# A Perceiver block with one core: splitting the first loads, moving late weights behind the query stores, and folding queries in runs of 1 KB

## The chip, the cores and the metric

One core of a Trainium2 chip runs the whole block in one launch. The metric is the device time of that launch in microseconds; the median of three runs is compared. The core's engines work side by side, each through its own instructions in order: PE (matrix products into PSUM banks, with PEld its weight load), DVE (vector work), ACT (functions and copies), POOL (here the reductions over partitions) and SP, which issues most of the DMAs. An engine waits for another only through semaphores. DMAs of one issuing order are kept to eight lanes: a DMA waits until the eighth before it has landed.

## The reference, cut to what matters

```python
def _L0_xattn_ref(query, context, w_q, w_kv, w_out, b_out):
    q = query @ w_q
    k, v = jnp.split(context @ w_kv, 2, axis=-1)
    ...
    scores = jnp.einsum('bhqd,bhkd->bhqk', q, k) * SCALE
    attn = jax.nn.softmax(scores, axis=-1)
    out = jnp.einsum('bhqk,bhkd->bhqd', attn, v)
    ...
    return out @ w_out + b_out
...
x = x + _L0_xattn_ref(_layernorm(x, axis=-1), ctx_768, ...)
x = x + _L0_attn_ref(_layernorm(x, axis=-1), ...)
x = x + _L0_ffn_ref(_layernorm(x, axis=-1), ...)
```

x is 32 x 64 x 256, the context 32 x 1601 x 192, with 16 heads of 64. The second term is a time mixing (three products with Wk, Wv and Wr, a scan over the 64 steps with a decay per channel, a product with Wo), the third a feed-forward net of width 1024. All is float32.

## The kernel before, in words

**Folded queries.** The key weights are not applied to the context. They are folded into the queries: for each head the query (64 numbers) is multiplied by the head's key weights (192 x 64), so that scores are products of a folded query with the raw context, over 192 channels. The setup makes these folded queries for all 32 batch rows and stores them in DRAM (q_dram, 25.2 MB). It works on four groups of eight rows (512 tokens). For each group, `queries` normalises x (statistics L110, xn L177), transposes it (xnT), and then for each pair of head pairs makes the queries on PE (q_ps L195), has ACT scale them into qT (L202), multiplies them by the turned key weights wkT (ql_ps L211 for the first 128 channels, qh_ps L226 for the other 64), has DVE and ACT copy the results to q_lo and q_hi (L218, L219, L233, L234) and issues their stores on SP (L236, L242). q_lo and q_hi have two buffers each.

**Loads of the setup.** SP issues first x_sb's tiles 0 to 3 (L91), then the key weights wk_lo and wk_hi in halves, the other tiles of x_sb, the first context's blocks cb (twelve DMAs, L153), and then everything that is used later: the value weights wv_lo and wv_hi, wo_sb, the four time-mixing weights nat_*, biases and per-channel columns (L281 to L298). ACT issues the two halves of wq_sb (L275). The time-mixing weights are turned on PE at the end of the setup (L320) and copied by DVE (L325), and the decay rows are made there (L327 to L332).

**Halves.** After the setup a loop runs over 64 halves u: batch row b = u // 2 and half of the heads j = u % 2. Half u computes its scores (`scores`: six groups of 24 s_ps matmul rows, L466, into two banks, each group copied to s_sb by ACT, L473, with a running maximum on DVE, L475 and L477; then a rest, L485) and the maximum over all keys (L495 and L496 on DVE, then a reduction on POOL, L503). Then come, for the half before it, the products of its probabilities with the context (`av_lo`, o_lo L569, thirteen steps; `av_hi`, o_hi L583), then the subtraction of the maximum (L513, DVE) and the exponential (L514, ACT) of its own scores, in four parts. So the exponentials of one half are covered by PE's products of the half before. The first half has none before it: its parts are put into the score loop of half 1 as hooks (L673), behind the copies of groups 2, 3, 4 and 5.

**Context.** `ctx_prep` turns the blocks cb of the next row into cT on DVE (L260, L261) and moves a part of it by DMA (L262); `ctx_load` loads the plain context c (L133, L136), and `q_load` the folded queries of a row (L163). `fill` names work that is put between steps of `av_lo`.

The kernel is written against a framework that assigns each instruction its place in its engine's order by a plan of its own; the order of the text is a priority, not the final order. Pools give memory out in the order in which they are opened: what is opened after the setup takes the setup's memory, and waits for its last readers.

Of the kernel before, what the change touches and what calls it, by code (L numbers as in the profile page):

```python
# [9 lines left out]
F32 = mybir.dt.float32  # L10
AF = mybir.ActivationFunctionType
ALU = mybir.AluOpType
# [3 lines left out]
P = 128  # L16
# [4 lines left out]
def kernel(  # L21
# [35 lines left out]
    nc = tc.nc  # L57

    B, T, D = x.shape
    NK, C = ctx_768.shape[1:]  # L60
# [30 lines left out]
    nc.sync.dma_start(x_sb[:, 0:4, :], xr[:, 0:4, :])  # L91
# [25 lines left out]
    with ExitStack() as st_b:  # L117
        with ExitStack() as st_a:
            kp = st_a.enter_context(tc.tile_pool(name="keys", bufs=2))
            cpool = st_a.enter_context(tc.tile_pool(name="ctx", bufs=1))  # L120
            aw = st_a.enter_context(tc.tile_pool(name="aw", bufs=1))
            wv_lo = aw.tile([P, INNER], F32, name="wv_lo")
            wv_hi = aw.tile([P, INNER], F32, name="wv_hi")
            wo_sb = aw.tile([P, INNER // P, D], F32, name="wo_sb")
# [44 lines left out]
            def queries(tg, sp, sps, wq_sb, wkT):  # L169
# [19 lines left out]
                for g in range(NP // 2):  # L189
                    qT = sp.tile([P, 2, TG], F32, tag="qT", name=f"qT_{tg}_{g}", bufs=6)  # L190
                    for k in range(2):
                        hp = 2 * g + k
                        pq = sps.tile([P, TG], F32, tag="ps", name=f"q_ps_{tg}_{hp}")
                        for c in range(2):
                            nc.tensor.matmul(  # L195
                                pq,
                                lhsT=wq_sb[:, c, hp * P : (hp + 1) * P],
                                rhs=xnT[:, c, :],
                                start=(c == 0),
                                stop=(c == 1),  # L200
                            )
                        nc.scalar.activation(qT[:, k, :], pq, AF.Copy, scale=HD**-0.5)  # L202
                    lo = sp.tile([P, QB, 4, T], F32, tag="q_lo", name=f"q_lo_{tg}_{g}", bufs=2)
                    hi = sp.tile([P, QB, 2, T], F32, tag="q_hi", name=f"q_hi_{tg}_{g}", bufs=2)
                    for k in range(2):
                        pl = [
                            sps.tile([P, QB, T], F32, tag="f", name=f"ql_ps_{tg}_{g}_{k}_{o}", bufs=6)
                            for o in range(2)
                        ]
                        for o in range(2):  # L210
                            nc.tensor.matmul(  # L211
                                pl[o],
                                lhsT=wkT[o * HD : (o + 1) * HD, 2 * g + k, 0:P],
                                rhs=qT[o * HD : (o + 1) * HD, k, :],
                                start=True,
                                stop=True,
                            )
                        nc.vector.tensor_copy(lo[:, :, 2 * k, :], pl[0])  # L218
                        nc.scalar.copy(lo[:, :, 2 * k + 1, :], pl[1])  # L219
                    ph = [  # L220
                        sps.tile([P, QB, T], F32, tag="f", name=f"qh_ps_{tg}_{g}_{o}", bufs=6)
                        for o in range(2)
                    ]
                    for k in range(2):
                        for o in range(2):
                            nc.tensor.matmul(  # L226
                                ph[o][k * C2 : (k + 1) * C2, :, :],
                                lhsT=wkT[o * HD : (o + 1) * HD, 2 * g + k, P:C],
                                rhs=qT[o * HD : (o + 1) * HD, k, :],
                                start=True,  # L230
                                stop=True,
                            )
                    nc.vector.tensor_copy(hi[:, :, 0, :], ph[0])  # L233
                    nc.vector.tensor_copy(hi[:, :, 1, :], ph[1])  # L234
                    ns = slice(4 * g * T, (4 * g + 4) * T)
                    nc.sync.dma_start(  # L236
                        q_dram[tg][:, 0:P, ns].rearrange("b p n -> p b n"),
                        lo.rearrange("p b h t -> p b (h t)"),
                    )
                    for k in range(2):  # L240
                        ns = slice((4 * g + 2 * k) * T, (4 * g + 2 * k + 2) * T)
                        nc.sync.dma_start(  # L242
                            q_dram[tg][:, P:C, ns].rearrange("b p n -> p b n"),
                            hi[k * C2 : (k + 1) * C2].rearrange("p b h t -> p b (h t)"),
                        )
# [19 lines left out]
            with tc.tile_pool(name="setup", bufs=1) as sp, tc.tile_pool(  # L265
# [7 lines left out]
                for n in range(2):  # L273
                    ns = slice(n * INNER // 2, (n + 1) * INNER // 2)
                    nc.scalar.dma_start(wq_sb[:, :, ns], wqr[:, :, ns])  # L275
                    nc.sync.dma_start(wk_lo[:, ns], w_kv[0:P, ns])
                    nc.sync.dma_start(wk_hi[:, ns], w_kv[P:C, ns])
# [3 lines left out]
                nc.sync.dma_start(wv_lo, w_kv[0:P, INNER : 2 * INNER])  # L281
                for r0 in (0, C2):
                    nc.sync.dma_start(wv_hi[r0 : r0 + C2, :], w_kv[P:C, INNER : 2 * INNER])
                nc.sync.dma_start(wo_sb, w_out.rearrange("(c p) n -> p c n", p=P))
                nats = {}
                for n, w in (("Wk", Wk), ("Wv", Wv), ("Wr", Wr), ("Wo", Wo)):
                    nats[n] = sp.tile([P, 2, D], F32, name=f"nat_{n}")
                    nc.sync.dma_start(nats[n], w.rearrange("(c p) h -> p c h", p=P))
                for n, v in enumerate((b_out, bo, b2)):
                    nc.sync.dma_start(bias_rows[:, n, :], v.partition_broadcast(P))  # L290
                with nc.allow_non_contiguous_dma(reason="per-channel vectors"):
                    for n, v in enumerate((time_decay, time_first)):
                        nc.sync.dma_start(cols[:, n, :], v.rearrange("(c p) -> p c", p=P))
                    for n, v in enumerate((mix_k, mix_v, mix_r)):
                        nc.sync.dma_start(
                            cols[:, 2 + n, :], v.rearrange("a b (c p) -> p (a b c)", p=P)
                        )
                    nc.sync.dma_start(b1_sb, b1.rearrange("(c p) -> p c", p=P))  # L298

# [16 lines left out]
                for n, nat in nats.items():  # L316
                    ps = sps.tile([P, 2, D], F32, tag="ps", name=f"rw_ps_{n}")
                    for hc in range(2):
                        for oc in range(2):
                            nc.tensor.transpose(  # L320
                                ps[:, hc, oc * P : (oc + 1) * P],
                                nat[:, oc, hc * P : (hc + 1) * P],
                                ident,
                            )
                    nc.vector.tensor_copy(rw_T[n], ps)  # L325

                nc.vector.tensor_scalar(omm, cols[:, 2:5, :], -1.0, 1.0, ALU.mult, ALU.add)  # L327
                nc.scalar.activation(td, cols[:, 0, :], AF.Exp)
                nc.scalar.activation(td, td, AF.Exp, scale=-1.0)
                for c in range(2):  # L330
                    nc.vector.tensor_scalar(
                        td_rows[:, c, :], ones, td[:, c : c + 1], None, ALU.mult  # L332
                    )

# [5 lines left out]
            def bank(shape, name):  # L340
                return ps_m.tile(shape, F32, tag="m", name=name)

# [315 lines left out]
            for u in range(2 * B):  # L658
# [5 lines left out]
                if phase == 1 and i >= 0:  # L664
                    fill = {2: [out.yproj], 6: [older.out] if i else []}
                elif phase == 2 and i >= 0:
                    fill = {6: [mixer.mix]}
                elif phase == 3 and i >= 0:
                    fill = {3: [mixer.project], 9: [mixer.gate]}

                if u == 1:

                    hooks = {i + 2: [part] for i, part in enumerate(parts)}  # L673
                elif last is not None:
                    hooks = {3: [last.inverse]}
                    last.total()
                else:
                    hooks = {}
# [4 lines left out]
                mb = max_all(u, mx)  # L683
                if last is not None:
                    last.av_lo(fill)
# [6 lines left out]
                if j == 0 and b + 1 < B:  # L692
                    cT_next = ctx_prep(b + 1)
                elif j == 1:
                    cT = cT_next
# [154 lines left out]
```

## Time and profile before

| | us |
|---|---|
| runs | 2626.71, 2626.44, 2626.01; median 2626.44 |
| profiled execution, its own time | 2624.3 |
| its span | 2622.5, mean granted clock 0.997 |
| first matmul on PE | 8.91 |
| first q_ps matmul | 17.04 |
| first store of q_lo issued | 38.77 |
| last store of q_hi issued (L242) | 139.60, over 1.57 |
| first copy of scores to s_sb | 147.40 |
| last qh_ps matmuls of the setup | 132.36, over 1.09 |
| first o_lo matmul | 186.44 |

The profile lists an operation as line, engine, operation, output and input tile, shape and count, with the busy time, the mean of one in ns and what ended the engine's idle time before it. Start times are from the start of the span. "SPq" stands for the queue of SP: the time that it needs to issue a DMA. From issue to landing the stores took 8.6 us (q_lo, 1 MB) and 6.8 us (q_hi, 256 KB) in the median. A group of transposes of a time-mixing weight (L320, four of 128 x 128) took 0.60 to 0.89 us on PE, a copy of the result (L325) 0.69 us on DVE.

### The profile page before, as it was taken

How to read it: one execution, taken by the hardware profiler on the slowest of the kernel's cores; microseconds unless marked ns; L12 is line 12 of the kernel's file. 1: busy time of each engine (PE TensorE's matmuls, PEld its weight loads, DVE VectorE, ACT ScalarE, POOL GpSimd, SP SyncE). 2: the span in 40 equal slices, each digit the busy share in tenths (PEclk: the TensorE clock that was granted, in tenths of full speed). 3: DMA queues.
4: the chain of work that ended last, by engine and by line, in shares of the span. 5: the costliest groups of instructions: out<-in, count | busy, mean ns of one | idle time of the engine just before them, and what ended most of it. 6: DMA issues, size and time to landing. Idle time of an engine off the chain costs nothing.

```text
span 2622.5 us, 28521 instructions
## 1 busy us (share of the span) xinstructions
PE 2593.2 (99%) x11456; PEld 1217.1 (46%) x11456; DVE 1907.2 (73%) x2283; ACT 953.6 (36%) x1019; POOL 355.3 (14%) x176
## 2 busy tenths in 40 slices
PE   8989999999999999999999999999999999999999
PEld 3334444444444444444444444444444444444466
DVE  4458878777787878777787868777787868787741
ACT  2333334333333334343433333343433334343221
POOL 0011111111111111111111111111111111111100
PEclk9989999999999999999999999999999999999999
DMA  8983333233322323333331313333331323310100
GB/s 202 284 162 57 56 51 63 44 63 63 63 57 49 63 39 63 44 63 63 63 63 44 63 39 63 46 61 63 63 63 44 63 45 57 59 29 20 51 11 23
DMA packets 437781, 169.33 MB, mean 65 GB/s; under 512 B 332400, under 2 KB 423952, under 8 KB 437648
## 3 DMA queue, kind: packets, MB, share of 16 engines
q1 hardware_dynamic: 437104, 166.46, 32.9%
q8 instruction: 90, 1.47, 0.3%
q10 hardware_dynamic: 544, 1.05, 0.1%
q14 instruction: 43, 0.35, 0.0%
HBM read 138.60 MB, written 27.26 MB: 63 GB/s over the span
## 4 chain that ended last, share of the span: by engine, by line
PE 96%; DMA 2%; SPq 1%; DVE 1%; POOL 0%; issue 0%; ACT 0%; DVEq 0%; POOLq 0%; ACTq 0%
PE s_ps L466 37%; PE o_lo L569 28%; PE o_hi L583 13%; PE s_ps_r L485 3%; PE fy L775 2%; PE v_ps L629 2%; PE y_ps L642 2%; PE h_ps L761 2%; PE q_ps L195 2%; PE o_hi L593 1%; PE ql_ps L211 1%; DMA q_dram<-q_lo 1%; PE Wv_ps L383 1%; PE Wr_ps L383 1%; PE Wk_ps L383 1%; DMA q_dram<-q_hi 1%
## 5 line engine op out<-in xcount | busy, mean ns | idle before, releaser
L466 PE MATMUL s_ps<-q,cT 64*128 64x512 f32 x4608 | 1011.3, 594 | 8.6 <-ACT s_sb L473 7.8
L569 PE MATMUL o_lo<-s_sb,c 128*128 128x512 f32 (+1 forms) x1664 | 743.5, 596 | 0.0
L473 ACT COPY s_sb<-s_ps 128x1024 f32<-128x1024 f32 x384 | 388.6, 1012 | 958.6 <-PE s_ps L466 945.5
L466 PEld LDWEIGHTS s_ps<-q,cT 64*128 64x128 f32 x4608 | 442.6, 188 | 548.9 <-issue 537.9
L514 ACT ACTIVATE s_sb<-s_sb 128x2048 f32<-128x2048 f32 (+1 forms) x256 | 398.6, 1585 | 466.0 <-DVE s_sb L513 466.0
L513 DVE TENSOR_TENSOR s_sb<-s_sb,mb 128x2048 f32<-128x2048 f32 (+1 forms) x256 | 471.6, 1886 | 101.9 <-POOL mb L503 101.9
L569 PEld LDWEIGHTS o_lo<-s_sb,c 128*128 128x128 f32 (+1 forms) x1664 | 307.5, 190 | 358.1 <-issue 350.8
L477 DVE TENSOR_TENSOR m<-m,s_sb 128x1024 f32<-128x1024 f32 x256 | 313.6, 1225 | 180.1 <-ACT s_sb L473 168.2
L583 PE MATMUL o_hi<-s_sb,c 128*64 128x512 f32 x1536 | 342.9, 595 | 0.0
L546 POOL PARTITION_ALL_REDUCE den<-sum x64 | 207.4, 3240 | 834.9 <-DVE oT L609 673.2
L540 DVE TENSOR_TENSOR t<-t,s_sb 128x1024 f32<-128x1024 f32 x256 | 310.5, 1213 | 4.0
L503 POOL PARTITION_ALL_REDUCE mb<-mx x64 | 114.2, 1785 | 906.7 <-DVE mx L496 788.7
L583 PEld LDWEIGHTS o_hi<-s_sb,c 128*64 128x64 f32 x1536 | 105.3, 137 | 220.0 <-issue 197.2
L556 DVE STREAM_TRANSPOSE turned<-den 128x512 f32<-128x512 f32 x64 | 45.5, 711 | 221.3 <-POOL den L546 221.3
L485 PE MATMUL s_ps_r<-q,cT 64*65 64x256 f32 x768 | 93.6, 376 | 0.0
L260 DVE STREAM_TRANSPOSE cT<-cb 128x768 f32<-128x768 f32 x96 | 92.7, 967 | 0.0
L475 DVE TENSOR_TENSOR m<-s_sb 128x1024 f32<-128x1024 f32 x64 | 75.8, 1184 | 10.3 <-ACT s_sb L473 10.3
L485 PEld LDWEIGHTS s_ps_r<-q,cT 64*65 64x65 f32 x768 | 54.0, 134 | 52.8 <-issue 33.5
L538 DVE TENSOR_TENSOR t<-s_sb 128x1024 f32<-128x1024 f32 x64 | 77.5, 1211 | 0.0
L102 POOL TENSOR_TENSOR rstd_ln<-rstd_ln,root 128x1 f32<-128x1 f32 (+1 forms) x24 | 31.3, 1304 | 276.5 <-DVE rstd_ln L101 276.5
L195 PE MATMUL q_ps<-xnT,wq_sb 128*128 128x512 f32 x128 | 61.0, 616 | 0.0
L642 PE MATMUL y_ps<-wo_sb,outT 128*128 128x256 f32 x256 | 58.0, 379 | 0.0
(111 smaller groups left out, 1507.4 us busy)
## 6 DMA issues: line engine op xcount, KB each, us to landing
q<-q_dram SPq DMA_DIRECT2D x64, 768.0 KB, 6.6
c<-in_ctx_dram SPq DMA_DIRECT2D x32, 1152.0 KB, 6.2
cb<-in_ctx_dram SPq DMA_DIRECT2D x192, 104.0 KB, 4.2
cb<-in_ctx_dram SPq DMA_DIRECT2D x192, 96.0 KB, 3.3
q_dram<-q_lo SPq DMA_DIRECT2D x16, 1024.0 KB, 8.6
q_dram<-q_hi SPq DMA_DIRECT2D x32, 256.0 KB, 6.8
x_sb<-in_x_dram SPq DMA_DIRECT2D x4, 512.0 KB, 9.7
w_sb<-in_L_ffn_w_dram SPq DMA_DIRECT2D x2, 1024.0 KB, 5.0
```

The costliest lines, as they stand in the source:

```text
L195: nc.tensor.matmul(pq, lhsT=wq_sb[:, c, hp * P : (hp + 1) * P], rhs=xnT[:, c, :], start=(c == 0), stop=(c == 1),)
L466: nc.tensor.matmul(ps[:, k, :], lhsT=cT[rs, s, i * P : (i + 1) * P], rhs=q[rs, s, js : js + HALF], start=(s == 0), stop=(s == NS - 1),)
L473: nc.scalar.copy(s_sb[:, 2 * i : 2 * i + 2, :], ps)
L477: nc.vector.tensor_tensor(m2, m2, s_sb[:, 2 * i : 2 * i + 2, :], ALU.max)
L485: nc.tensor.matmul(ps[0:KR, k, 0:HH], lhsT=cT[rs, s, NB1 * BL : KT + 1], rhs=q[rs, s, js + k * HH : js + (k + 1) * HH], start=(s == 0), st ...
L503: nc.gpsimd.partition_all_reduce(mb, mx, P, bass_isa.ReduceOp.max)
L513: nc.vector.tensor_tensor(s, s, m, ALU.subtract)
L514: nc.scalar.activation(s, s, AF.Exp)
L540: nc.vector.tensor_tensor(t2, t2, p[:, 2 * i : 2 * i + 2, :], ALU.add)
L546: nc.gpsimd.partition_all_reduce(self.den, self.sum, P, bass_isa.ReduceOp.add)
L569: nc.tensor.matmul(self.po, lhsT=self.ctx[0:n, self.at[c], 0:P], rhs=self.s_sb[0:n, c, :], start=(c == 0), stop=(c == NCK - 1),)
L583: nc.tensor.matmul(self.ph[o * C2 : (o + 1) * C2, :], lhsT=self.ctx[:, self.at[c], P:C], rhs=self.s_sb[:, c, :], start=(c < 2), stop=False ...
```

## The change

1. **First loads.** x_sb's tiles 0 to 3 are loaded in two halves, one on SP and one on ACT, between the first and the second half of the key weights; wk_hi and half of wq_sb move between the queues too.
2. **Folded queries.** Two pairs of head pairs are handled together: four query products, then the two q_lo, then one q_hi of twice the size, whose runs in DRAM are 1 KB instead of 512 B. There are half as many stores of q_hi.
3. **Late loads.** Value weights, wo_sb, time-mixing weights, biases and columns are issued after the setup's block in the text. Their pool is opened there, so wv_lo, wv_hi and wo_sb take memory of the setup. The time-mixing weights are loaded as halves into tiles of the time mixing.
4. **Weights turned.** The four time-mixing weights are turned in `av_lo` of half 1 (the fill of u = 2, behind steps 2, 5, 8 and 11), and copied by ACT instead of DVE. The decay rows are named in the fill of u = 3.
5. **First exponentials.** The hooks of half 1 move to the copies of groups 3, 4 and 5 (the last has two parts). `ctx_prep(1)` moves from half 0 behind the maximum of half 1.

```diff
-    nc.sync.dma_start(x_sb[:, 0:4, :], xr[:, 0:4, :])
...
-                for g in range(NP // 2):
-                    qT = sp.tile([P, 2, TG], F32, tag="qT", name=f"qT_{tg}_{g}", bufs=6)
+                for e in range(NP // 4):
+                    hi = sp.tile([P, QB, 4, T], F32, tag="q_hi", name=f"q_hi_{tg}_{e}", bufs=2)
+                    qTs = []
+                    for g in (2 * e, 2 * e + 1):
+                        qT = sp.tile([P, 2, TG], F32, tag="qT", name=f"qT_{tg}_{g}", bufs=6)
+                        qTs.append(qT)
...
+                    for g, qT in zip((2 * e, 2 * e + 1), qTs):
+                        lo = sp.tile([P, QB, 4, T], F32, tag="q_lo", name=f"q_lo_{tg}_{g}", bufs=2)
...
-                    nc.vector.tensor_copy(hi[:, :, 0, :], ph[0])
-                    nc.vector.tensor_copy(hi[:, :, 1, :], ph[1])
...
                         for o in range(2):
...
+                            nc.vector.tensor_copy(hi[:, :, 2 * k + o, :], ph[o])
+                    for n in range(2):
+                        ns = slice((8 * e + 4 * n) * T, (8 * e + 4 * n + 4) * T)
                         nc.sync.dma_start(
                             q_dram[tg][:, P:C, ns].rearrange("b p n -> p b n"),
-                            hi[k * C2 : (k + 1) * C2].rearrange("p b h t -> p b (h t)"),
+                            hi[n * C2 : (n + 1) * C2].rearrange("p b h t -> p b (h t)"),
                         )
...
-                for n in range(2):
-                    ns = slice(n * INNER // 2, (n + 1) * INNER // 2)
-                    nc.scalar.dma_start(wq_sb[:, :, ns], wqr[:, :, ns])
+                halves = [slice(n * INNER // 2, (n + 1) * INNER // 2) for n in range(2)]
+                for n, ns in enumerate(halves):
                     nc.sync.dma_start(wk_lo[:, ns], w_kv[0:P, ns])
-                    nc.sync.dma_start(wk_hi[:, ns], w_kv[P:C, ns])
+                    nc.scalar.dma_start(wk_hi[:, ns], w_kv[P:C, ns])
+                    if n == 0:
+                        nc.sync.dma_start(x_sb[:, 0:2, :], xr[:, 0:2, :])
+                        nc.scalar.dma_start(x_sb[:, 2:4, :], xr[:, 2:4, :])
+                for eng, ns in zip((nc.sync, nc.scalar), halves):
+                    eng.dma_start(wq_sb[:, :, ns], wqr[:, :, ns])
...
+            aw = st_a.enter_context(tc.tile_pool(name="aw", bufs=1))
...
+            nc.sync.dma_start(wv_lo, w_kv[0:P, INNER : 2 * INNER])
...
+            tags = iter(("xn", "in_k", "in_v", "in_r", "e", "ev", "num", "den"))
...
+                nats[n] = [rp.tile([P, D], F32, tag=next(tags), name=f"nat_{n}_{c}") for c in range(2)]
...
+            def turn(n):
+
+                ps = bank([P, 2, D], f"rw_ps_{n}")
+                for hc in range(2):
+                    for oc in range(2):
+                        nc.tensor.transpose(
+                            ps[:, hc, oc * P : (oc + 1) * P],
+                            nats[n][oc][:, hc * P : (hc + 1) * P],
+                            ident,
+                        )
+                nc.scalar.copy(rw_T[n], ps)
+
+            def decay():
                 nc.vector.tensor_scalar(omm, cols[:, 2:5, :], -1.0, 1.0, ALU.mult, ALU.add)
                 nc.scalar.activation(td, cols[:, 0, :], AF.Exp)
                 nc.scalar.activation(td, td, AF.Exp, scale=-1.0)
...
                 fill = {}
-                if phase == 1 and i >= 0:
+                if u == 2:
+                    fill = {c: [lambda n=n: turn(n)] for c, n in zip((2, 5, 8, 11), nats)}
+                elif u == 3:
+                    fill = {6: [decay]}
+                elif phase == 1 and i >= 0:
...
-                    hooks = {i + 2: [part] for i, part in enumerate(parts)}
+                    hooks = {3: parts[0:1], 4: parts[1:2], 5: parts[2:]}
...
                 mb = max_all(u, mx)
+                if u == 1:
+                    cT_next = ctx_prep(1)
...
-                if j == 0 and b + 1 < B:
+                if j == 0 and 0 < b < B - 1:
                     cT_next = ctx_prep(b + 1)
```

## The prediction

> **What bounds the kernel now.** I read the page's busy shares first, then PE's waits over the first 190 us, then the windows of 10 us and the timeline of the head.
>
> ```profile
> PE 2593.2 (99%) x11456; PEld 1217.1 (46%) x11456; DVE 1907.2 (73%) x2283; ACT 953.6 (36%) x1019; POOL 355.3 (14%) x176
> ...
> PE wkT_ps L304 <- DMA wk_lo<-in_L_xattn_w_kv_dram: 8.9, 1, 8.9
> PE s_ps L466 <- ACT s_sb L473: 7.8, 2, 7.1
> PE rw_ps_Wr L320 <- DVE Wk_T L325: 2.9, 1, 2.9
> ```
>
> PE is busy in all but 29 us of the 2622.5 us span. The chain of waits is PE without a break from 175.26 us on, 34.03 us for each of the 64 halves plus their fills. The changed program keeps the order of PE, ACT, POOL and SP from the fifth half on, so only the head can move.
>
> ```profile
> 70.00:80.00 10.00, 9.70 (x42) 3.48 (x40) 5.15 (x8) 2.74 (x5) 0.00 (x0) 1.00 0.99 296
> 80.00:90.00 10.00, 8.96 (x36) 3.06 (x36) 4.22 (x8) 2.65 (x5) 0.00 (x0) 1.00 0.99 300
> ...
> 170.00:180.00 10.00, 4.74 (x14) 2.15 (x16) 9.85 (x8) 6.73 (x6) 0.00 (x0) 0.66 0.99 120
> ```
>
> The last three columns are granted clock, DMA share, GB/s. The folded queries are bound by their stores (DMA 0.99 busy, some 298 GB/s), and PE only looks busy. These stores start late:
>
> ```profile
> 13.75 0.75 DVE L110 BATCH_NORM_STATS2 st_ln<-x_sb 128x6 f32<-128x256 f32 x2 [0.78 <-DMA x_sb<-in_x_dram]
> 17.04 4.56 PE L195 MATMUL q_ps<-xnT,wq_sb 128*128 128x512 f32 x8
> 38.77 0.49 SPq L236 DMA_DIRECT2D q_dram<-q_lo  x1
> 147.40 1.93 ACT L473 COPY s_sb<-s_ps 128x1024 f32<-128x1024 f32 x2 [13.10 <-DMA cb<-in_ctx_dram]
> 175.26 9.95 PE L466 MATMUL s_ps<-q,cT 64*128 64x512 f32 x36 [7.12 <-ACT s_sb L473]
> 232.81 1.91 ACT L514 ACTIVATE s_sb<-s_sb 128x2048 f32<-128x2048 f32 x1 [11.63 <-DVE s_sb L513]
> ```
>
> The first q_lo was evacuated at 24.8 us but is issued at 38.77, behind the weights on SP. At 147.40 ACT may write s_sb, once the last store has landed: call this moment T0. All later steps of the head hang on T0; PE resumes at 175.26 = T0 + 27.86.
>
> **The start (first loads split over SP and ACT).** Weights reach PE earlier, but in the changed program DVE takes the statistics of x_sb tile 4 ahead of the first xn (L177). That load landed at 13.7 us and stands behind the same 2.8 MB (half of x_sb's first tiles, wk, wq, itself) in both kernels. From 13.7: statistics 0.39, three xn 1.0, two wkT copies 1.2, xn and statistics 0.75, to 17.1; PE turns the other two wkT pairs (1.4 each) only after those copies, to 18.55; last wkT copy to 19.15; xnT 0.95; its copy to 20.45. So q_ps starts at 20.5 instead of 17.04. If the load comes at 11 us, at 17.8. I take 19.9: 2.9 later.
>
> **The folded queries (two pairs at a time, 1 KB runs, late loads behind the stores).** Now a store can leave as soon as it is evacuated, near 30 us. PE's rows for one of four groups: 32 q_ps at 0.436, 32 ql_ps at 0.24, 32 qh_ps at 0.128, xnT 1.9: 27.6 us. Four are 110.4; less the first xnT, plus 0.9 for the slow first matmuls and 0.2 at each later xnT, 110: PE ends at 129.9. Stores are 25.2 MB, at 298 GB/s 84.5 us; queries back 7, time-mixing weights and biases 4.5, per-channel columns 1.5, four cb loads 3.2: 101 us from 31, at 132. A group's stores (21.1 us) fit under its 27.6 of PE, with q_lo's two buffers giving 4 us more, so PE sets the pace. I add 1.0: the decay chain (L328, L332), hoisted by the order into the fourth group, makes ACT and DVE wait for the columns, which SP issues behind the third group's stores and a landing each; queued there are the q_lo and q_hi evacuations, and PE for their banks. PE ends at 130.9.
>
> The last 3.15 MB take 10.6 us. The first of them is evacuated 3.2 us before PE's end and moves 1.5 later; biases, columns and three cb loads before it cost 1.4: T0 = 130.9 + 10.3 = **141.2**, 6.2 earlier. Bounds: 136 (early x_sb, no backlog) to 146 (PE waiting for stores as before).
>
> The Trainium skill (DMA: Bandwidth & Descriptors, Specifications) says that 512 B already suffices for line rate, so by it the longer runs give nothing; the trace, with both sizes mixed at 0.99 busy, can't part them. If a 512 B packet cost as much as one of 1 KB, the tail's 3,072 packets would take their share of 32,768 in 84.5 us, 7.9, and end 2.7 earlier.
>
> **Exponentials behind the fourth copy.** The hooks say so; the built order does not. On ACT the second half's first copy is followed by three exponentials, then its second copy (before: two). PE has two score banks and waits for that second copy. The transposes of cT (L260) now leave the subtractions in one piece: first subtraction at T0 + 18.1 (19.0 before), three at 2.2, the third exponential 1.91, the copy 0.99: T0 + 27.85. Before: 27.86. So **0**; had the hooks held, up to 7.1.
>
> **Loads after T0.** wv_lo, wv_hi and wo_sb (2.1 MB) wait for every store, then go ahead of eight of the next context's twelve cb loads, q, and c. DVE's cT transpose stands between the two steps of the maximum (L495, L496) and needs the tenth cb; behind it are the maximum, POOL's reduction, every exponential. 2.1 MB at 300 GB/s from T0 + 1.9, six cb at 0.8 (1.28 MB at 128 GB/s around 216 to 226 us): T0 + 13.7, needed at T0 + 14.5. So 0, the cover being 0.8 us. Bounds: 0 to 7.2 (195 GB/s as at 24 to 26 us, and cb's median landing of 4.2 on top: T0 + 21.7). c lands near T0 + 26, needed at T0 + 39.
>
> **Weights turned amid low sums.** In the setup they hid under the stores. Now 16 transposes stand in o_lo of the second half, PE-bound: two cost 0.22 in a later fill (5.15 + 6.21 + 0.22), so 16 cost 1.8. Two banks serve four weights: the fourth turn waits for Wv_T's copy, behind the third half's first exponential on ACT. That ended at 234.72, T0 + 87.3; with DVE 0.8 earlier and the copy of 0.6, T0 + 87.1. PE is there at T0 + 85.0 (o_lo from T0 + 73.1, twelve steps of 0.874, three turns). So 2.1 of stall: **+3.9**. Bounds 1.8 to 6.0. DVE loses four copies, ACT gains them, both with room.
>
> The 7.12 us wait was followed by a granted clock of 0.66, and a group of scores took 4.7 instead of 2.58. The Trainium skill (TensorE: Matmul & The Clock Gate, What's actually happening) puts the clock down after an idle window of about 3.4 us; by that 2.1 stays free, by the row's effect it would cost 2.1 more.
>
> **Sum.** Against the profiled run's 2624.3 (span 2622.5): -6.2 + 0 + 0 + 3.9 = -2.3, 2622.0. The runs' median, 2626.44, is 2.1 above that execution, so I forecast **2624.2**.
>
> **Rivals.**
> - A, faster: stores and PE overlap as meant. x_sb tile 4 comes by 11 us (-2.1), no backlog (-1.4), stores of 1 KB faster at the tail (-2.7), fourth turn partly covered (-1): 2617.0. For: the DMA stands near idle at 50 to 60 us now. Against: the order on DVE and SP.
> - B, slower: cb behind wv and wo_sb. Place: the transpose between L495 and L496; price 7.2: 2631.4, above the median as soon as the tenth cb lands later than T0 + 16.7. For: cb moves at 128 GB/s, and its lanes wait for those loads' landings. Against: HBM loads reach 350 GB/s at 32 to 36 us.
> - C, the hooks act after all: 7.1 less, 2617. The order speaks against it.
> - D, stores still set T0 at 147.4: 2624.2 + 6.2 = 2630.4. Against: 101 us of DMA from 31.
>
> **Chances.** A change is told from none beyond 0.2%, 5.3 us: 2621.2 and 2631.7. Forecast 0.48, within; A 0.32 and C 0.02, faster; B 0.12 and D 0.06, of each about half beyond 2631.7, when the turn is at its bound too (2.1 more). Faster 0.34, same 0.57, slower 0.09. Range 2618 to 2630.5 (from A's nearer part to D); the forecast's own is 2621 to 2629.
>
> **What would show it.** First q_ps near 20, first store near 30, first s_sb copy near 141, PE idle some 7 us before the second half's fourth score group, PE waiting about 2 us at the last weight's turn, the first subtraction 18 us after the first copy. The sum is wrong if T0 is below 138 or the maximum waits for cb.

## The result and the profile after

The changed kernel takes 2625.15 us (median of 14 runs, 2624.04 to 2627.08), the kernel before 2625.84 in as many runs beside it (2623.45 to 2629.73). The ratio is 0.9997 with an interval of 0.9989 to 1.0006: no difference that can be told. The forecast was 2624.2.

The profiled execution of the changed kernel took 2625.9, its span is 2624.1. The page's busy shares, as before engine, busy us, share and instructions:

```profile
PE 2587.6 (99%) x11456; PEld 1217.6 (46%) x11456; DVE 1904.9 (73%) x2279; ACT 957.2 (36%) x1023; POOL 355.4 (14%) x176
```

PE's waits over the whole span of the changed kernel (who waited for whom: total us, times, longest):

```profile
PE s_ps L478 <- ACT s_sb L485: 11.4, 2, 7.6
PE wkT_ps L289 <- DVE wkT L293: 7.0, 1, 7.0
...
PE qh_ps L231 <- ACT q_lo L218: 1.5, 1, 1.5
...
PE rw_ps_Wo L339 <- ACT Wv_T L344: 1.0, 1, 1.0
```

The wait for the turned weight in the setup (2.9 before) is gone. The wait of the scores for ACT is still there, 7.6 in one piece, and has a second part of 3.9. New are, above all, the 7.0 for the wkT copy at the start and the 1.0 for the last weight's bank; smaller ones are new as well (1.5 behind a copy of q_lo, and 3.0 in three pieces behind copies of xnT).

Windows of the changed kernel, with the same columns as before (granted clock, DMA share and GB/s last):

```profile
70.00:80.00 10.00, 8.70 (x43) 3.77 (x40) 7.30 (x14) 2.54 (x6) 0.00 (x0) 1.00 1.04 316
80.00:90.00 10.00, 10.00 (x43) 3.79 (x42) 4.67 (x8) 4.13 (x7) 0.00 (x0) 1.00 0.95 271
...
170.00:180.00 10.00, 6.74 (x18) 2.92 (x20) 9.87 (x11) 5.35 (x6) 0.00 (x0) 0.54 0.80 141
```

The DMA is still nearly full in the middle of the setup, and the stretch behind the 7.6 us wait still runs at about half the clock. The moments that the forecast named, in the timeline (start, busy, engine, line, operation, in brackets the idle time and who ended it):

```profile
13.71 0.43 DVE L109 BATCH_NORM_STATS2 st_ln<-x_sb 128x6 f32<-128x256 f32 x1 [4.66 <-DMA x_sb<-in_x_dram]
...
20.31 8.06 PE L194 MATMUL q_ps<-xnT,wq_sb 128*128 128x512 f32 x16
...
31.09 2.08 SPq L220 DMA_DIRECT2D q_dram<-q_lo  x2
...
143.25 1.93 ACT L485 COPY s_sb<-s_ps 128x1024 f32<-128x1024 f32 x2 [11.22 <-DMA q_dram<-q_hi]
148.90 1.01 ACT L485 COPY s_sb<-s_ps 128x1024 f32<-128x1024 f32 x1 [3.73 <-PE s_ps L478]
...
165.99 1.91 ACT L526 ACTIVATE s_sb<-s_sb 128x2048 f32<-128x2048 f32 x1 [4.40 <-DVE s_sb L525]
168.19 1.91 ACT L526 ACTIVATE s_sb<-s_sb 128x2048 f32<-128x2048 f32 x1 [0.29 <-DVE s_sb L525]
170.40 1.91 ACT L526 ACTIVATE s_sb<-s_sb 128x2048 f32<-128x2048 f32 x1 [0.29 <-DVE s_sb L525]
172.21 0.99 ACT L485 COPY s_sb<-s_ps 128x1024 f32<-128x1024 f32 x1
...
173.26 10.94 PE L478 MATMUL s_ps<-q,cT 64*128 64x512 f32 x36 [7.57 <-ACT s_sb L485]
...
232.39 0.66 PE L339 MATMUL rw_ps_Wo<-ident,nat_Wo 128*128 128x128 f32 x4 [1.05 <-ACT Wv_T L344]
```

DVE stands 4.66 us for x_sb's fifth tile, and three exponentials stand on ACT between the second half's first copy (160.58) and its second (172.21), which is what PE waits for. Both are as the built order said.

| moment, us | before | forecast | after |
|---|---|---|---|
| first q_ps | 17.04 | 19.9 | 20.31 |
| first q_lo store issued | 38.77 | near 30 | 31.09 |
| PE's end of the folded queries | 133.45 | 130.9 | 133.25 |
| T0, first copy of scores | 147.40 | 141.2 | 143.25 |
| T0 to the first subtraction | 19.0 | 18.1 | 20.35 |
| T0 to PE's resumption in half 1 | 27.86 | 27.85 | 30.01 |
| T0 to o_lo of half 0 | 39.04 | 39.04 | 42.17 |
| o_lo of half 1 to scores of half 3 | 17.10 | 21.0 | 20.11 |
| scores of half 3 | 237.57 | 235.3 | 239.57 |

### The profile page after: what moved, and what is told of

Read it like the earlier page. It is cut to its first block, busy times and chain, and to the rows that moved or that the text cites. A ratio compares the mean times of both kernels' runs of the same rounds, so it can differ in the third digit from the quotient of the medians.

```text
span 2624.1 us, 28498 instructions
## 1 busy us (share of the span) xinstructions
PE 2587.6 (99%) x11456; PEld 1217.6 (46%) x11456; DVE 1904.9 (73%) x2279; ACT 957.2 (36%) x1023; POOL 355.4 (14%) x176
## 3 DMA queue, kind: packets, MB, share of 16 engines
q10 hardware_dynamic: 704, 1.05, 0.1%
## 4 chain that ended last, share of the span: by engine, by line
PE 96%; DVE 1%; DMA 1%; SPq 1%; POOL 0%; issue 0%; ACT 0%; DVEq 0%; POOLq 0%; ACTq 0%
PE s_ps L478 37%; PE o_lo L581 27%; PE o_hi L595 13%; PE s_ps_r L497 3%; PE fy L793 2%; PE v_ps L641 2%; PE y_ps L654 2%; PE h_ps L779 2%; PE q_ps L194 2%; PE o_hi L605 1%; PE ql_ps L210 1%; PE Wv_ps L395 1%; PE Wk_ps L395 1%; PE Wr_ps L395 1%; PE qh_ps L231 1%; PE ry L456 0%
## 5 line engine op out<-in xcount | busy, mean ns | idle before, releaser
L478 PE MATMUL s_ps<-q,cT 64*128 64x512 f32 x4608 | 1011.3, 594 | 13.2 <-ACT s_sb L485 11.4
```

Of the source, the lines that this page charges most:

```text
L478: nc.tensor.matmul(ps[:, k, :], lhsT=cT[rs, s, i * P : (i + 1) * P], rhs=q[rs, s, js : js + HALF], start=(s == 0), stop=(s == NS - 1),)
```

## The experiments

All runs start from the changed kernel; diffs are against it. `issue_after` and `keep_in_program_order` fix an instruction's place in its engine's order. T0 and span are those of each profiled execution, which can lie anywhere among the runs of its kernel; the median is that of all of them (5 to 14). Ratios are against the kernel before, run beside each kernel; its medians there were 2625.84 to 2626.59, so the medians of two rows compare to some 0.75 us.

| kernel | T0 | span | median | ratio, interval |
|---|---|---|---|---|
| the changed kernel | 143.25 | 2624.1 | 2625.15 | 0.9997, 0.9989 to 1.0006 |
| start | 140.11 | 2621.0 | 2625.00 | 0.9993, 0.9985 to 1.0002 |
| decay | 140.85 | 2621.3 | 2623.97 | 0.9993, 0.9984 to 1.0002 |
| turn | 144.70 | 2622.2 | 2622.00 | 0.9979, 0.9970 to 0.9988 |
| hooks | 143.96 | 2626.3 | 2627.79 | 1.0002, 0.9994 to 1.0011 |
| runs of 512 B | 148.12 | 2628.6 | 2630.16 | 1.0014, 1.0005 to 1.0023 |
| runs of 512 B, decay | 144.74 | 2627.7 | 2629.50 | 1.0014, 1.0005 to 1.0023 |
| buffers apart | 137.70 | 2622.9 | 2623.96 | 0.9992, 0.9983 to 1.0001 |
| buffers apart, value weights last | 138.96 | 2618.8 | 2619.28 | 0.9974, 0.9964 to 0.9983 |
| start, decay, turn | 139.80 | 2616.9 | 2618.41 | 0.9970, 0.9958 to 0.9981 |
| start, decay, turn, hooks | 138.99 | 2612.2 | 2615.59 | 0.9961, 0.9947 to 0.9974 |
| all of these | 133.63 | 2608.1 | 2609.24 | 0.9936, 0.9924 to 0.9949 |
| all, sum of half 1 later | 133.28 | 2601.4 | 2603.45 | 0.9914, 0.9900 to 0.9927 |

### The start

```diff
-                mv, rstd = stats_of(sp, [tg * NX + k for k in range(NX)], f"ln1_{tg}")
+                with tc.issue_after(turned[0]) if tg == 1 else ExitStack():
+                    mv, rstd = stats_of(sp, [tg * NX + k for k in range(NX)], f"ln1_{tg}")
...
-                    nc.vector.tensor_copy(xnT[:, c, :], pt)
+                    turned[0] = nc.vector.tensor_copy(xnT[:, c, :], pt).ins
```

(The exponentials are also held behind the second half's first copy, where they stood, so that ACT's order stays.)

> The changed kernel, with the statistics of the second group's x tiles queued on DVE behind the first group's xnT copies. Theory (the forecast's step on the start): the statistics of x_sb tile 4 hold up the first xn, so q_ps starts near 17 instead of 20.3, PE ends the setup 3.3 us earlier, T0 (first copy of scores) comes near 140.0 instead of 143.25, and the time falls by 3.3. Rival: the later part of the setup waits for stores or columns, not for PE: q_ps starts earlier, T0 stays within 1 us of 143.25, and the time moves by less than 1.

q_ps started at 16.9 instead of 20.31, PE ended the folded queries at 130.09 instead of 133.25 and T0 came 3.14 earlier (140.11); the span is 3.1 shorter. The trace has the theory's numbers. DVE's timeline in this run (columns as above) shows the xn without the wait:

```profile
10.27 1.38 DVE L175 TENSOR_SCALAR xn<-x_sb,mv_ln,rstd_ln 128x256 f32<-128x256 f32 x4 [1.22 <-POOL rstd_ln L101]
11.57 1.01 DVE L296 COPY wkT<-wkT_ps 128x384 f32<-128x384 f32 x2
```

But this execution is the fastest of the eleven. The medians differ by 0.15 only, where 3.3 was expected, and the intervals overlap widely: the step is shown in the trace, its worth in the time of this run alone is not.

### The decay chain

```diff
-                nc.vector.tensor_scalar(omm, cols[:, 2:5, :], -1.0, 1.0, ALU.mult, ALU.add)
-                nc.scalar.activation(td, cols[:, 0, :], AF.Exp)
+                tc.keep_in_program_order(
+                    nc.vector.tensor_scalar(omm, cols[:, 2:5, :], -1.0, 1.0, ALU.mult, ALU.add)
+                )
+                tc.keep_in_program_order(nc.scalar.activation(td, cols[:, 0, :], AF.Exp))
```

> The changed kernel, with the decay chain (omm, td, td_rows) held at its named place in the program, after the copies of the fourth half's scores. Theory: in the fourth query group ACT and DVE stood behind the late columns, and PE behind them: PE ends the setup 1.5 to 2.5 us earlier than 133.25, T0 likewise, the time falls by 2. Rival: that wait had slack, the group is held by its stores: T0 moves by less than 0.5 and the time does not change.

PE ended at 128.94, 4.3 earlier, more than expected; T0 came 2.4 earlier, as expected. The median fell by 1.2, with intervals that overlap: as with the start, the step is shown in the trace and not in the time. What had cost this in the changed kernel is on ACT's timeline there:

```profile
112.12 0.59 ACT L218 COPY q_lo<-ql_ps 128x512 f32<-128x512 f32 x1 [0.54 <-PE ql_ps L210]
116.11 0.20 ACT L348 ACTIVATE td<-cols 128x2 f32<-128x2 f32 x1 [3.41 <-DMA cols<-n_L_attn_time_decay_dram]
...
116.46 1.54 ACT L218 COPY q_lo<-ql_ps 128x512 f32<-128x512 f32 x3
```

The copies of q_lo stood 3.41 us behind two tiny exponentials that waited for a column of 1 KB. DVE waited 3.01 for the same result, PE 1.51 for a bank, and then ran a stretch at a lower clock (0.89 in 110 to 120). The forecast had 1.0 for all this.

### The turn

```diff
-                if u == 2:
-                    fill = {c: [lambda n=n: turn(n)] for c, n in zip((2, 5, 8, 11), nats)}
-                elif u == 3:
+                if u == 3:
...
+            for n in nats:
+                turn(n)
             c_tiles = {}
```

(The first scores are kept behind the turns on PE, the exponentials and ctx_prep(1) at their places on ACT and DVE.)

> The changed kernel, with the four time-mixing weights turned on PE between the last folded query and the first scores, while the last stores land, instead of in o_lo of the second half. Theory: their 3.0 us in o_lo (16 transposes and the stall at the fourth) go, and in the idle 10 us after the setup they cost nothing: o_lo(1) to scores(3) takes 17.1 instead of 20.1, the time falls by 3.0, and by up to 1 more if PE's clock starts higher at the first scores. Rival: the four copies on ACT or the transposes delay the first scores by as much, or half of the 3.0 us was not the transposes: less than 1.5 off.

The turns took 136.0 to 138.5 on PE, while the stores landed. From o_lo of half 1 to the scores of half 3 PE took 17.09 instead of 20.11: 3.0, the whole price of the turns. The median fell by 3.15. The span fell by 1.9 only, because T0 came 1.45 later in this execution, the slowest of its eleven. The order of the setup is the same, and PE had ended the folded queries 0.96 later already, ahead of the turns; that is how far two executions of one setup lie apart.

### The hooks

```diff
-                    nc.scalar.copy(s_sb[:, 2 * i : 2 * i + 2, :], ps)
+                    done = nc.scalar.copy(s_sb[:, 2 * i : 2 * i + 2, :], ps)
...
                     for hook in hooks.get(i, ()):
-                        hook()
+                        with tc.issue_after(done.ins):
+                            hook()
```

> The changed kernel, with each exponential of the first half really queued on ACT behind the score copy that its hook names (first behind the fourth copy, second behind the fifth, the rest behind the sixth); nothing else changes its place on PE or SP. Theory (the forecast's): the hooks had no effect in the changed kernel, and PE's 7.57 us wait for the second copy of the second half is theirs to remove. Then PE runs from the third to the fourth score group without a stop, its clock stays near 1.0 in 165 to 180 us, and o_lo of the first half starts near 175 instead of 185.4: 7 to 10.6 us off the time, some 2615 to 2618. Rival: the wait only moves to the next place, because the exponentials end near 178 instead of 172.3 and o_lo waits for them or for the c tile: o_lo starts at 180 or later, at most 5 us off. Second rival: the order on ACT is not what the trace shows, then nothing changes.

The first half of the theory held to the number, and the time did not move. PE's timeline with the hooks:

```profile
158.42 15.70 PE L478 MATMUL s_ps<-q,cT 64*128 64x512 f32 x72
173.96 1.46 PE L498 MATMUL s_ps_r<-q,cT 64*65 64x256 f32 x12
175.35 11.43 PE L582 MATMUL o_lo<-s_sb,c 128*128 128x512 f32 x26
...
231.26 1.11 PE L339 MATMUL rw_ps_Wo<-ident,nat_Wo 128*128 128x128 f32 x4 [9.35 <-ACT Wv_T L344]
...
234.01 7.42 PE L596 MATMUL o_hi<-s_sb,c 128*64 128x512 f32 x24
```

and DVE's and ACT's where that last wait comes from:

```profile
216.51 1.19 DVE L487 TENSOR_TENSOR m<-s_sb 128x1024 f32<-128x1024 f32 x1
...
228.83 1.91 ACT L527 ACTIVATE s_sb<-s_sb 128x2048 f32<-128x2048 f32 x1 [14.89 <-DVE s_sb L526]
230.64 0.57 ACT L344 COPY Wv_T<-rw_ps_Wv 128x512 f32<-128x512 f32 x1
```

The scores of half 1 run through, o_lo of half 0 starts at 175.35 instead of 185.42, 10 us earlier. All of it is handed back at the fourth turn: 9.35 us of waiting, and o_hi behind it takes 7.42 instead of 5.37. Wv_T's copy stands on ACT behind the third half's first exponential, which starts at 228.83. That one waits for DVE, which has worked since 164 with no more than waits for POOL's reductions (1.68, 3.13 and 3.02) and begins the third half's maximum at 216.51. Neither rival named this wait; the expectation's 7 to 10.6 us was a miss.

### Runs of 512 B

```diff
-                        ns = slice((8 * e + 4 * n) * T, (8 * e + 4 * n + 4) * T)
-                        nc.sync.dma_start(
-                            q_dram[tg][:, P:C, ns].rearrange("b p n -> p b n"),
-                            hi[n * C2 : (n + 1) * C2].rearrange("p b h t -> p b (h t)"),
-                        )
+                        for k in (0, 2):
+                            h0 = 8 * e + 4 * n + k
+                            nc.sync.dma_start(
+                                q_dram[tg][:, P:C, h0 * T : (h0 + 2) * T].rearrange("b p n -> p b n"),
+                                hi[n * C2 : (n + 1) * C2, :, k : k + 2, :].rearrange(
+                                    "p b h t -> p b (h t)"
+                                ),
+                            )
```

> The changed kernel with each store of q_hi as two of half the heads, runs of 512 B instead of 1 KB, as before the change; PE, DVE and ACT keep their order. Theory 1 (stores cost by bytes): GB/s stays near 334 in 134 to 138 us, T0 moves by less than 0.5, the time by less than 0.5. Theory 2 (a packet of 512 B costs nearly what one of 1 KB does): the last stores take longer, T0 comes up to 2.7 later, the DMA share between 30 and 130 us rises, and the time grows by 1 to 3.

5.0 slower in the median: more than either theory had. (The edit changes two things: the runs are half as long, and there are twice as many stores of q_hi.) T0 came at 148.12, but the last stores took no longer than before (10.4 behind PE's end, 10.0 in the changed kernel); PE itself ended 4.5 later, with a wait of 4.74 in the fourth group, where the columns were issued at 116.19 instead of 112.21. So it looked as if the whole price came through the decay chain. The next run asked that: the same edit, with the decay chain out of the way.

> The kernel with q_hi in runs of 512 B, and the decay chain at its named place as well. With 512 B alone the time grew by 5 us; there SP issued the columns at 116.19 instead of 112.21 us, and PE waited 4.7 us in the fourth query group. Theory: most of what the 1 KB runs are worth comes through this wait; without the decay chain in the fourth group, T0 comes within 1 us of the 140.85 that the decay edit alone had, and the span within 1.5 us of its 2621.3. Rival: the stores themselves take longer and set the end of the setup: T0 143 or later, span 2623.5 or more.

That theory fell. PE now ended at 129.01, as without the 512 B (128.94), and still T0 came 3.9 later than with the decay edit alone. The packets and SP's queue of DMAs (q1) in 70 to 110 us, and SP's last stores of q_hi, first for the decay edit with 1 KB:

```profile
DMA packets 10971, 11.72 MB, mean 293 GB/s; under 512 B 762, under 2 KB 10585, under 8 KB 10968
...
q1 hardware_dynamic: 10968, 11.68, 98.9%
...
130.64 2.65 SPq L242 DMA_DIRECT2D q_dram<-q_hi  x2
```

and for the same with 512 B:

```profile
DMA packets 12981, 11.25 MB, mean 281 GB/s; under 512 B 798, under 2 KB 12593, under 8 KB 12977
...
q1 hardware_dynamic: 12977, 11.20, 95.6%
...
132.68 6.86 SPq L243 DMA_DIRECT2D q_dram<-q_hi  x4
```

The second run moved 4% fewer bytes per us, though q_hi is only a third of the stores' bytes. Over the 110 us from the first store to T0 that is 4 to 5 us; T0 moved by 3.9. But its DMA engines were also less busy: 95.6% of the time instead of 98.9%. Per busy time the queue moved 293 and 295 GB/s (an estimate: 11.20 and 11.68 MB in 40 us, divided by these shares), the same within 1%. So the packets of 512 B did not move their bytes more slowly, and theory 2 falls. The Trainium skill (DMA: Bandwidth & Descriptors, Specifications) puts the smallest transfer for line rate at 512 B, which agrees.

What the trace shows instead is engines that stood idle longer, and a slower issue. SP's queue needed 6.86 us for the last four stores of q_hi where it had needed 2.65 for two with the same bytes, and issued the last one at 137.5 instead of 131.9. Whether this comes from the number of stores or from the length of their runs stays open: no run has 512 B in as few stores. (The span moved by 6.4, more than T0, because in this execution the fourth turn's stop was 2.51, where the decay run had 1.28, and o_hi behind it took 7.07 us instead of 5.37. The median moved by 5.5.)

### The buffers apart

```diff
             with tc.tile_pool(name="setup", bufs=1) as sp, tc.tile_pool(
-                name="setup_ps", bufs=2, space=PSUM
-            ) as sps:
+                name="stage", bufs=2
+            ) as stage, tc.tile_pool(name="setup_ps", bufs=2, space=PSUM) as sps:
...
-                        lo = sp.tile([P, QB, 4, T], F32, tag="q_lo", name=f"q_lo_{tg}_{g}", bufs=2)
+                        lo = stage.tile([P, QB, 4, T], F32, tag="q_lo", name=f"q_lo_{tg}_{g}", bufs=2)
...
+            ae = st_a.enter_context(tc.tile_pool(name="even", bufs=1))
             ap = st_a.enter_context(tc.tile_pool(name="attn", bufs=1))
...
-                s_sb = ap.tile([P, NCK, HALF], F32, tag="s_sb", name=f"s_sb_{u}", bufs=2)
+                s_sb = (ap if u % 2 else ae).tile([P, NCK, HALF], F32, tag="s_sb", name=f"s_sb_{u}")
```

(q_hi goes into the new pool as well, m2 and mx into "even".)

> The changed kernel with the q_lo and q_hi buffers in a place of their own, away from the first half's s_sb, m2 and mx: the first copy of scores then waits for PE's last folded query and no longer for the landing of the last stores; the value weights are issued as soon as PE is done too. Theory: T0 (the 10 us behind PE's end in the forecast) is only this reuse of a buffer: T0 comes at 138 to 139 instead of 143.25, and everything behind it with it, the time falls by 4 to 5. Rival (the forecast's rival B): the next context's blocks, behind the stores and 2.1 MB of weights in the same queue, do not come earlier; DVE's transpose ahead of the end of the maximum waits for the tenth block, the first subtraction stays within 1.5 us of 163.6, and the time falls by less than 2.

T0 came at 137.70, 4.8 behind PE's end instead of 10.0, and the first copy now waits for PE's scores instead of a DMA: the wait at T0 was this reuse of memory. And the rival was right about the rest. ACT's first copy and DVE's timeline in this run:

```profile
137.70 1.01 ACT L486 COPY s_sb<-s_ps 128x1024 f32<-128x1024 f32 x1 [6.00 <-PE s_ps L479]
...
152.75 0.69 DVE L508 TENSOR_TENSOR mx<-m 128x512 f32<-128x512 f32 x1
158.72 0.98 DVE L260 STREAM_TRANSPOSE cT<-cb 128x768 f32<-128x768 f32 x1 [5.28 <-DMA cb<-in_ctx_dram]
159.63 0.64 DVE L509 TENSOR_TENSOR mx<-mx,s_sb 65x512 f32<-65x512 f32 x1
...
162.41 4.50 DVE L526 TENSOR_TENSOR s_sb<-s_sb,mb 128x2048 f32<-128x2048 f32 x2 [1.24 <-POOL mb L516]
```

The transpose between the two steps of the maximum waits 5.28 us for a block, and the first subtraction comes 1.2 earlier instead of 5.5. In the changed kernel the same transpose waited 0.31, so the forecast's rival B stood there with its cover just used up. The next run takes the 2.1 MB from ahead of the blocks:

```diff
-            nc.sync.dma_start(wv_lo, w_kv[0:P, INNER : 2 * INNER])
...
                     c_tiles[b] = ctx_load(b)
+                if u == 0:
+                    nc.sync.dma_start(wv_lo, w_kv[0:P, INNER : 2 * INNER])
...
```

> The kernel with q_lo and q_hi in a place of their own, and the value and output weights issued behind the next context's blocks, queries and c. With the place alone, T0 came at 137.7, but DVE's transpose waited 5.28 us for a block and the first subtraction came only at 162.4 (T0 + 24.7). Theory: the 2.1 MB ahead of the blocks made that wait; the first subtraction comes at T0 + 18 to T0 + 20 (156 to 158), PE resumes in the second half near 166 instead of 172.06, the span falls by 5 to 6 to 2617. Rival: the blocks are late because of the stores ahead of them, whatever stands between: first subtraction at 160 or later, gain under 2.5.

The transpose no longer waits, the first subtraction comes at T0 + 19.3 and PE resumes at 167.95 (T0 + 29.0). The median falls by 4.7 to 2619.28. The theory holds: the value weights made that wait, not the stores. (The span falls by 4.1, less than the 5 to 6 expected, since T0 came 1.26 later in this execution.)

### The edits together

The diffs are those above. First start, decay and turn:

> The changed kernel with three of the earlier edits together: statistics behind the first xnT copies, decay chain at its named place, weights turned behind the last folded query. If the three losses are independent, T0 comes 3.1 (start) and 2.8 (decay) earlier than 143.25 or 144.7, near 137.5 to 139, T0 to scores(3) takes 93 instead of 96.3 us, and the span is 2615 to 2617, 8 us below the changed kernel's 2624.1. Rival: with both setup losses gone the stores set the pace, T0 stays above 139.5, and the span is 2618 to 2620.

The span is what the theory said, but not by its road. PE ended at 126.6 and T0 came at 139.80: 13.2 behind, so the stores now set it, as the rival had it, and of the 5.5 that the two setup edits brought one by one (3.1 and 2.4) 3.5 are left. From T0 to the scores of half 3 it took 92.55.

Then the hooks with them:

> The three edits of the sum and the exponentials held behind the fourth score copy. In the run with the hooks alone PE lost its 7.6 us wait and 10 us were gone by o_lo of the first half, but DVE, busy without a gap, reached the third half's maximum late, and PE waited 9.35 us at the fourth turn. Theory: the late engine is DVE, so without the turn the wait comes one place later, before the third score group of the fourth half, because the third half's exponentials on ACT end 92 us after T0: PE waits 4 to 5 us there and the gain over the sum is about 3 us (span 2612 to 2614). Rival: the turn's bank alone made the wait; then PE runs through and the gain over the sum is 9 to 10 us (2606). Second rival: nothing gained, within 1 us of the sum.

Now the hooks are worth 2.8 in the median, and the wait is where the theory put it, ahead of the third score group of half 3 (T0 + 92.1):

```profile
231.12 12.27 PE L483 MATMUL s_ps<-q,cT 64*128 64x512 f32 x48 [4.07 <-ACT s_sb L492]
```

DVE is the late engine; the turn had only been where it showed.

Then the buffers apart and the value weights last as well:

> All edits together: statistics behind the first xnT copies, decay chain at its named place, weights turned behind the last folded query, exponentials behind the fourth score copy, q_lo and q_hi in a place of their own, value weights behind the next context. Sum: T0 near 132 (PE's end of the setup near 126.6, and 5 as with the place alone) instead of 139.0, o_lo of the first half near 161.5 instead of 170.1, the wait of the fourth half's scores again to T0 + 92, then 34 us a half: span 2605 to 2606, 7 us below 2612.2. Rival: blocks or c come no earlier than the stores let them, and the gain is under 3 us (span over 2609).

Between the two: 4.1 off the span (2608.1, where 2605 to 2606 was expected), 6.3 off the median. PE runs from the turns to o_lo of half 0 without a stop, but that is 164.47, not 161.5, because the turns and two halves of scores on PE alone take until then. The 4.06 us wait in half 3 stayed. DVE's order gave the last edit: in half 2 the sum and the inverse of half 1 stood ahead of the maximum that the exponentials need.

```diff
+                elif u == 2:
+                    hooks = {}
                 elif last is not None:
                     hooks = {3: [last.inverse]}
                     last.total()
...
                 mb = max_all(u, mx)
+                if u == 2:
+                    with tc.issue_after(folds[1]):
+                        last.total()
+                        last.inverse()
```

(folds[1] is the first step of L495 in half 2.)

> All edits together, and the second half's sum and inverse on DVE moved from ahead of the third half's maximum to behind it. With all edits PE still waited 4.06 us ahead of the third score group of the fourth half (225.89), because DVE began the third half's maximum only at 205.79, 6 us after its last copy. Theory: DVE's order alone makes that wait; the third half's exponentials end near 218 instead of 224.9, PE runs through at 221.8, o_lo of the third half starts near 234.5 instead of 240.49, the span is near 2602. Rival: DVE has no room, the wait moves one half on (the fifth half's scores) and the span falls by less than 2.

PE's timeline of the last kernel around the place of that wait:

```profile
216.05 15.72 PE L480 MATMUL s_ps<-q,cT 64*128 64x512 f32 x72
231.60 1.46 PE L502 MATMUL s_ps_r<-q,cT 64*65 64x256 f32 x12
232.99 11.43 PE L588 MATMUL o_lo<-s_sb,c 128*128 128x512 f32 x26
```

The 72 score rows of half 3 (its six groups have twelve each, not 24) run in one piece; half 2's exponentials end at 216.8, before PE needs their engine. The theory holds, and the span is 2601.4, near its 2602. 2603.45 us is 0.9914 of the kernel before (0.9900 to 0.9927).

## Why the forecast came out

The time was right; its sum was right only in part. In the two profiled executions the steps add to +2.0 at the scores of half 3, where the forecast had -2.3. Some of this is the scatter of single executions: their own times differ by +1.6, the medians by -0.7, since before's profiled execution lies 1.5 under its 14-run median and the changed kernel's 0.75 above its own. That the medians come within 1 us of the forecast is so in part luck. The rest is in the steps:

- **Start.** Right in mechanism and nearly in size (19.9 forecast, 20.31 measured); the start run took it away and got 3.1 at T0.
- **Folded queries.** "I add 1.0" for the decay chain was the mis-sized term: without the chain T0 came 2.4 earlier and PE's end 4.3. The waits behind one late column were counted once, but they lie on ACT, DVE and PE in turn, and PE's clock falls behind them (0.89 in 110 to 120). The sum without the chain, 129.9, was 1.0 too long (128.94 in the decay run, with q_ps at 19.96), which hid a part of this. The step "T0 = 130.9 + 10.3" had the tail right (10.0), and the buffers apart show its cause. But the tail is no fixed length: with PE earlier it grew to 11.9 (decay) and 13.2 (start, decay, turn).
- **The 1 KB runs.** The forecast had 0 in the sum and up to 2.7 at the tail. Taking them back, with twice the stores of q_hi, cost 5.0 us in the median (3.9 at T0 with the chain out of the way): this part of the change held up the rest. The 2.7 had a 512 B packet cost as much as one of 1 KB; the trace shows nearly the same rate per busy time, and a slower issue on SP in every group (5.1 to 7.4 us for four stores) instead.
- **Behind T0.** Here the forecast wrote "So **0**" for the hooks, and they did nothing, as the order said. What it missed is 3.1 from T0 to o_lo of half 0. PE now stands 3.86 us between the second and third score group, where before it stood 0.67 and had its slow stretch ahead of T0. The third copy comes at T0 + 5.65 instead of T0 + 3.95 (1.7); in the start, decay and turn runs, with stops of 3.89, 5.78 and 1.94, it comes at T0 + 5.60 to 5.65 too (in start, decay, turn at T0 + 6.60, with the hooks as well at 5.36). The late block adds 0.31, and behind the 7.57 us stop the clock of 0.54 instead of 0.66 adds 1.0.
- **Turn.** 3.0 instead of 3.9: the stall was 1.05, not 2.1, because PE came later and the exponentials with it; the transposes took the rest. The turn run took both away at once; the split rests on the traces.
- **Rivals.** B was there at 0.31, and at 5.28 when T0 came at 137.70. C's price was wrong: the 7.1 of the hooks were 10 at o_lo of half 0 and nothing at the end, since DVE was next. A did not come: tile 4 landed only at 13.71, and its two parts in the setup, worth 3.1 (start) and 2.4 (decay) at T0 one by one, gave 3.5 together, since the stores were next. D did not come (143.25).

The lines behind the later third copy, PE's score groups of half 0 before:

```profile
139.72 8.07 PE L466 MATMUL s_ps<-q,cT 64*128 64x512 f32 x24 [0.83 <-issue]
148.46 10.57 PE L466 MATMUL s_ps<-q,cT 64*128 64x512 f32 x48 [0.67 <-ACT s_sb L473]
```

and after:

```profile
135.03 5.42 PE L478 MATMUL s_ps<-q,cT 64*128 64x512 f32 x24 [1.78 <-issue]
144.31 12.27 PE L478 MATMUL s_ps<-q,cT 64*128 64x512 f32 x48 [3.86 <-ACT s_sb L485]
```

What stays open: why T0 of one setup differs by 1.45 from one execution to the next, and what makes SP's issue slower with 512 B.

## What to carry to other kernels

A step that is ahead of time on one engine is worth only what the next engine can follow: after each wait that a change removes, ask which engine has had no room since then, and look for its late result two stages on. Small work that is ready "any time" (statistics of the next tiles, a chain on a few columns, a transpose for the next row) must be looked up in the built order, because in an in-order queue it makes everything behind it wait for its own DMA. And where new memory waits for old readers, the price of a tight layout is the landing of the last store; giving those buffers their own place pays only when the loads queued behind them are put in the order of need.

## What the runs showed of the hardware

- While the DMA engines were busy, the stream with a third of the stores' bytes in packets of 512 B moved as fast as the one with 1 KB alone (293 and 295 GB/s per busy time, an estimate from 11.20 MB at 95.6% and 11.68 MB at 98.9% in 40 us). Issuing was slower: in the median SP's queue needed 1.58 us for each of 32 stores of 256 KB in runs of 512 B, and 1.20 us for each of 16 stores of 512 KB in runs of 1 KB.
- PE's clock after a stop is not told by the stop's length alone. At the fourth turn, stops of 1.00, 1.05, 1.28, 1.59, 1.78 and 2.44 us left o_hi at 5.37 us; 2.51 made it 7.07 and 9.35 made it 7.42. In the turn run a stop of 1.94 between two score groups was followed by a clock of 0.57 for 4 us. The Trainium skill (TensorE: Matmul & The Clock Gate, What's actually happening) describes a free-running window of about 3.4 us, which fits that a place in time and not a length decides. If the windows are that long, a stop of 1.94 fills none of them, so a window with some work in it can take the clock down too.
